# Two PSUM banks for the quantised convolution, and a second issuer for the last image's transfers

## The chip, the cores and the metric

The kernel runs on one core of one Trainium2 chip. The time is device microseconds of one execution of the whole kernel. The core has five engines with instruction streams of their own: TensorE (PE in the profile; its weight loads are the row PEld), VectorE (DVE), ScalarE (ACT), GpSimd (POOL) and SyncE (SP). PE writes its results into PSUM, which here is handled as eight banks of 512 float32 per partition. Transfers between device memory (HBM) and on-chip memory (SBUF) run on 16 DMA engines and are started by an instruction on an engine's queue; in this kernel SP and POOL start them.

## The reference

The input is x, 32 images of 8 channels by 256 by 256 pixels, float32. Four layers follow each other, and each is added to its own input, normalised over groups of two channels:

```python
def _gn(v, G=4, eps=1e-5):
    g = v.reshape(B_, G, C_ // G, H_, W_)
    m = jnp.mean(g, axis=(2, 3, 4), keepdims=True)
    s = jnp.var(g, axis=(2, 3, 4), keepdims=True)
    return ((g - m) / jnp.sqrt(s + eps)).reshape(v.shape)

def _L0_conv_ref(x, K_local, Wp, bp, Wu, bu, Wg1, bg1, Wg2, bg2):
    drive = x[:, :C_OUT]
    grid = drive
    for _ in range(STEPS):                                   # 15
        mapped = R * grid * (1.0 - grid)
        local = _conv(mapped, K_local, groups=C_OUT)         # 3x3, each channel by itself
        physics = (1.0 - EPS) * mapped + EPS * local
        grid = (1.0 - BETA) * physics + BETA * drive
    cml_out = jnp.clip(grid, 0.0001, 1.0 - 0.0001)
    h = jax.nn.relu(_conv(x, Wp, bp))                        # 3x3, 8 -> 128 channels
    nca_out = jax.nn.sigmoid(_conv(h, Wu, bu))               # 1x1, 128 -> 8
    gin = jnp.concatenate([x, cml_out, nca_out], axis=1)     # 24 channels
    g = jax.nn.sigmoid(_conv(jax.nn.relu(_conv(gin, Wg1, bg1)), Wg2, bg2))
    return g * cml_out + (1.0 - g) * nca_out

def _L1_conv_ref(x, weight, bias):
    sx = MAX_Q / jnp.max(jnp.abs(x))                         # over all 32 images
    sw = MAX_Q / jnp.max(jnp.abs(weight))
    qx, qw = _quantize(x, sx), _quantize(weight, sw)         # round, clip to +-127
    return conv3x3(qx, qw) / (sx * sw) + bias[None, :, None, None]

x = x + _L0_conv_ref(_gn(x), ...)
x = x + _L1_conv_ref(_gn(x), ...)
x = x + conv3x3(_gn(x), weight2) + bias2                     # layer 2, 8 -> 8 channels
x = x + box5x5(_gn(x))                                       # layer 3, each channel by itself
```

Layer 1's scale is a maximum over all images after layer 0, so no image can enter layer 1 before the last one has left layer 0.

## The kernel before, in words

**The order is written by a planner.** The kernel builds a list of operations (class `Op`, L61) and gives each an engine, an estimated cost in us, the operations it comes after, a rank, and where needed a `Hold` (a number of PSUM banks that it takes; a later operation frees them) and a transfer size. `Plan.run` (L97) plays these through a small simulation of the five engines: an engine that comes free takes the ready operation of the lowest rank, PE the one of the lowest rank and due time whose banks are free. The order that comes out is the order in which each engine's instructions are written, layer 0 in one plan and layers 1 to 3 of all images in a second. A cost in an `add` call is therefore no instruction: it is an estimate that decides the order. What the chip then does is held in that order by each engine's queue, and between engines by semaphores.

**Layer 0 (to about 9411 us).** An image is worked on as four strips of 64 rows, and strip n = 4 x image + s. For each image 15 steps of the coupled map run on PE (L564), DVE (L587) and ACT (L666), and then:

- the clipped map is written to a buffer `cm_d` in HBM by 76 small stores (L708, through `pool_dma`, L390), 19 rows of tiles by two column sets by two parities, each of 5 to 8 rows of an exchange pattern;
- `hidden` (the 8 to 128 convolution): two loads of `zx` per strip (L770), eight groups of PE matmuls (L810), relu on ACT (L818) and DVE (L824), then the 1x1 convolution (L847, the operation `second`) and its sigmoid (L859) into `nh`, which four stores write to `nn_d` (L864);
- `gate`, one per strip: it reads four loads of `ci` (the map again, L897), `xc` (L908), two loads of `zg` (the input, L920), eight loads of `zc` from `cm_d` and eight of `zn` from `nn_d` (`load_z`, L737). Each load of `load_z` is 16 rows of 8316 bytes, with the source taken as 2 by 8 of them. Its three groups of matmuls (L954) take zg, zc and zn in this order; then relu, a 1x1 matmul, sigmoid, the mixing on DVE, statistics, and two stores to `x1_d`.

zc, zn, zg, ci and xc have one buffer each, so the loads of a gate begin when the gate before has released them. A gate of strip s needs nn of strips s - 1, s and s + 1. All transfers named here are issued by POOL. While the maps of earlier images run, strips of the image before fill the gaps; for the last image, 31, nothing comes after it, and layer 0 ends with its strips 124 to 127.

**Layers 1 to 3 (from about 9411 us).** An image lies in SBUF as 128 partitions of 16 rows. Image after image goes through

- `load1` (L1174): eight loads of x on POOL;
- `layer1`: four `shift` copies on ACT (L1239), rounding on DVE (L1135 and L1136), four `whole` copies on ACT (L1245) that write the rounded image `qh`; two transfers of neighbour rows `qb` on SP (`beside`, L1205); eight convolution groups `conv3` of one bank each (L1190 and L1194), each evicted on ACT into `x2` (L1273) and followed on DVE by the residual and `bn_stats` (L1285, L1294). I call these eight c0 to c7;
- `layer2`: group sums by two small PE operations and DVE work, among them `spread`; four transfers of neighbour rows `xb2` on SP (`beside` again, seen as `xb<-x` at L1205), one buffer of it for all images; four groups of products of two banks (L1367), here P.0 to P.3, evicted on ACT (L1379), statistics (L1391), and copies to a second layout `zz` on POOL (L1406, L1414);
- `layer3`: two groups of products on z and two and a part on zz (L1468, L1474), here Z and ZZ, evicted on ACT (L1493, L1499) into `o`, and 32 stores of `out` per image on SP (L1514).

Layers 1 and 2 take their banks from the first half of PSUM (banks 0 to 3), layer 3 from the second. In layer 1 a convolution group waits for `near` (the rounded image with its neighbour rows) and for the last readers of the `x2` buffer it will be evicted to, that of two images before:

```python
m = add(
    "PE", 0.9, lambda h=hold, i=i: conv3(slot(h), i), near + at_b(x2_used, b - 2),
    takes=hold,
)
```

Its eviction waits for the same readers. So up to four groups may be ahead of the evictions, as many as the half has banks. SP's queue carries in each image, in the order that the plan writes, two qb, the 32 stores of out of the image before, and four xb.

Of the kernel before, what the change touches and what calls it, by code (L numbers as in the profile page):

```python
# [19 lines left out]
C = 8  # L20
# [8 lines left out]
WS = W2 + 2  # L29
SC = WS * WS  # L30
# [175 lines left out]
def window(ap, offset, dims):  # L206
    return bass.AP(ap.tensor, ap.offset + offset, [list(d) for d in dims])
# [3 lines left out]
def kernel(  # L211
# [4 lines left out]
    nc = tc.nc  # L216
# [86 lines left out]
    with ExitStack() as es:  # L303
# [84 lines left out]
        def pool_dma(to, src, after, size, rank=1):  # L388
            return add(
                "POOL", 0.62, lambda: nc.gpsimd.dma_start(to(), src()), after, rank, size=size  # L390
            )

        def sp_dma(to, src, after, rank=0, size=0.2):
            return add(
                "SP", 0.58, lambda: nc.sync.dma_start(to(), src()), after, rank, size=size
            )


        stored_cm, free_a, free_s, set_of = {}, {}, {}, {}
        drive_b, drive_a, begun, tiles = {}, {}, {}, {}  # L400
# [225 lines left out]
        def steps(b):  # L626
# [67 lines left out]
            for q in range(4):  # L694
                cm_at[b][q] = []
                for i in range(5 if q < 3 else 4):
                    ready = [clipped[p, i // 3] for p in range(2)]
                    for e in range(2):
                        for par in range(2):
                            first, count = 2 - par, 7  # L700
                            if not par and q == i == 0:
                                first, count = 0, 8
                            if q and i == 0:
                                first, count = 6 - par, 5
                            if par and q == 3 and i == 3:
                                count = 8
                            at = 33 * q + 7 * i + (first + 1) // 2
                            cm_at[b][q].append(pool_dma(  # L708
                                lambda e=e, par=par, at=at, count=count: window(
                                    cm_d[b % 3], plane(e, par) + at * WS + 1 - e,  # L710
                                    [[WS, count], [SC, C], [1, wide]],
                                ),
                                lambda q=q, i=i, e=e, first=first, count=count: window(
                                    xb, (32 * q + 16 * (1 - e) + first) * row + i * WS,
                                    [[2 * row, count], [5 * WS, C], [1, wide]],
                                ),
                                ready + was, moving(8 * count, 516, 8),
                            ))
                stored_cm[b] += cm_at[b][q]
# [5 lines left out]
        def load_z(name, d, n, after):  # L725

            b, s = divmod(n, 4)
            out = []
            for r in range(2):
                for e in range(2):  # L730
                    for par in range(2):
                        def do(r=r, e=e, par=par):
                            if (r, e, par) == (0, 0, 0):
                                tiles[name, n] = zp.tile([P, 16, WS], F32, name=name, bufs=1)
                            at = 64 * r + 32 * e + 16 * par
                            z = tiles[name, n].rearrange("p s w -> p (s w)")
                            nc.gpsimd.dma_start(  # L737
                                z[at : at + 16, 0 : 16 * WS - 1],
                                window(
                                    d[b % 3], plane(1 - e, par) + (32 * s + 16 * r) * WS + e,  # L740
                                    [[WS, 2], [SC, C], [1, 16 * WS - 1]],
                                ),
                            )

                        out.append(add(
                            "POOL", 0.62, do, after + out[:1], size=moving(16, 8320)
                        ))
            return out

        def at_n(d, n):  # L750
# [10 lines left out]
        def hidden(n):  # L761
# [102 lines left out]
                closed.append(add("ACT", 0.69, close, [w], 0, frees=[hold]))  # L864
            was = [o for m in range(4 * (b - 3), 4 * (b - 2)) for o in at_n(nn_read, m)]
            for q in range(4):
                stored_nn[n].append(pool_dma(
                    lambda q=q: pairs(nn_d[b % 3], s, q), lambda q=q: nhs[n % 3][32 * q : 32 * q + 32],
                    closed + was, moving(256, 520),
                ))  # L870
            if s > 0:
# [16 lines left out]
        def gate(n):  # L888
# [2 lines left out]
            cms = [o for q in range(max(s - 1, 0), s + 1) for o in cm_at[b][q]]  # L891
            ci = []
            for q in range(4):
                def load_ci(q=q):
                    if q == 0:
                        tiles["ci", n] = hp.tile([P, 8, WS], F32, name="ci", bufs=1)
                    nc.gpsimd.dma_start(  # L897
                        tiles["ci", n][32 * q : 32 * q + 32], pairs(cm_d[b % 3], s, q)
                    )

                ci.append(add(
                    "POOL", 0.62, load_ci, cms + at_n(gate_done, n - 1) + ci[:1],
                    size=moving(256, 520),
                ))

            def load_xc():
# [185 lines left out]
    with ExitStack() as es:  # L1092
# [141 lines left out]
        def layer1(b, loaded):  # L1234
            near = []
            for k in range(4):
                def shift(k=k):
                    tiles["tq", b, k] = two.tile([P, 1024], F32, name="tq")
                    nc.scalar.activation(  # L1239
                        tiles["tq", b, k], tiles["x1", b][:, bass.ts(k, 1024)], AF.Identity,  # L1240
                        bias=less1[:, b : b + 1], scale=stat1[:, b, 1:2],
                    )

                def whole(k=k):
                    nc.scalar.activation(  # L1245
                        window(
                            qh, 4 * k * WP + 1, [qh.ap[0], [1, 2], [WP, 4], [2, W2]],
                        ),
                        tiles["tq", b, k].rearrange("p (e i w) -> p e i w", e=2, w=W2),
                        AF.Copy, bias=-ROUND,  # L1250
                    )

                a = add("ACT", 1.1, shift, loaded[k] + at_b(tq_used, 0)[-2:-1] + shifts[-1:])
                shifts.append(a)
                a = add("DVE", 1.55, lambda k=k: round_off(tiles["tq", b, k], sc[:, 0:1]), [a])
                a = add("ACT", 1.1, whole, [a] + at_b(qh_used, b - 1) + at_b(tq_used, 0)[-1:])
                tq_used.setdefault(0, []).append(a)
                near.append(a)
            near += beside(lambda: qb, lambda: qh, ((0, RB - 1, -1), (24, 0, 1)), near, 0.95)
            qh_used[b] = []  # L1260
            ops, last = [], None
            for i in range(NCH):
                hold = Hold(1, 0)
                m = add(
                    "PE", 0.9, lambda h=hold, i=i: conv3(slot(h), i), near + at_b(x2_used, b - 2),
                    takes=hold,
                )
                qh_used[b].append(m)

                def evict(h=hold, i=i):  # L1270
                    if i == 0:
                        tiles["x2", b] = two.tile([P, HB, WP], F32, name="x2")
                    nc.scalar.activation(  # L1273
                        tiles["x2", b][:, 2 * i : 2 * i + 2, 1 : 1 + W],
                        slot(h).rearrange("p (k w) -> p k w", w=W), AF.Identity, bias=b1_sb,
                        scale=sc[:, 3:4],
                    )

                def rest(i=i):
                    if i == 0:  # L1280
                        part_sums[1, b] = few.tile([P, HB, 6], F32, name="bn1")
                    x1, x2 = tiles["x1", b], tiles["x2", b]
                    c = x2[:, 2 * i : 2 * i + 2, 1 : 1 + W]
                    by = window(x2, 2 * i * WP + 1, [x2.ap[0], [1, 2], [WP, 2], [2, W2]])
                    nc.vector.tensor_tensor(  # L1285
                        by, by,
                        window(
                            x1, 1024 * (i // 2) + 2 * W2 * (i % 2),
                            [x1.ap[0], [512, 2], [W2, 2], [1, W2]],
                        ),  # L1290
                        ALU.add,
                    )
                    for n in range(2):
                        nc.vector.bn_stats(part_sums[1, b][:, 2 * i + n, :], c[:, n, :])  # L1294

                last = add("ACT", 0.8, evict, [m, last] + at_b(x2_used, b - 2), 0, frees=[hold])
                ops.append(add("DVE", 1.6, rest, [last] + ops[:1]))
            x1_used[b] = ops
            return sums_of(1, b, ops)
# [120 lines left out]
        def layer3(b, s, a, copies):  # L1420
# [32 lines left out]
            for n in range(2):  # L1453
# [54 lines left out]
                for d in range(4):  # L1508
                    for ro in range(4):
                        u = 1 if n == 1 and d == 0 and ro < 2 else 0  # L1510
                        r = 8 * d + (-2 if n else 2) + ro + 32 * u
                        mine.append(add(
                            "SP", 0.42,
                            lambda n=n, d=d, ro=ro, u=u, r=r: nc.sync.dma_start(  # L1514
                                window(
                                    out, (b * C * H + r) * W, [[H * W, C], [32 * W, 8], [1, W]]
# [252 lines left out]
```

## Time and profile before

| | |
|---|---|
| time, median of 3 runs | 11946.05 us (11938.4 to 11969.75) |
| the profiled execution's own time, and its span | 11955.15 us, 11953.3 us |
| layer 0, layers 1 to 3 | to about 9411 us, 9411 to 11953 us |
| busy share of the span: PE, PEld, DVE, ACT, POOL | 82%, 36%, 57%, 47%, 35% |
| PE in the slices of layer 0, of layers 1 to 3 | eight tenths or nine, five or six tenths |
| granted TensorE clock, mean | 0.921 |
| DMA queues: POOL's (q0), SP's (q1) | 1256.7 MB, 277.6 MB |

The profile is of one execution. Its time is 9.1 us above the median of the three runs, so a sum made from the profile is compared with 11955.15 and then shifted. Times within the profile count from the start of the span. In the lines of a timeline stand the start, the length, the engine (SPq is SP's queue), the source line, the operation, what it writes and reads, the tile's shape and count, and in brackets the idle time of the engine before it with what ended it. In the windows view the columns are the window, its length, then for PE, PEld, DVE, ACT and POOL the busy time with the number of instructions, then the granted clock, the busy share of the DMA engines and their GB/s. In the view of waits stand what is waited for, the sum in us, the number of waits and the longest of them.

### The profile page before, as it was taken

What the parts mean: (1) busy time and instruction counts of PE and PEld (TensorE: products, weight loads), DVE (VectorE), ACT (ScalarE), POOL (GpSimd) and SP (SyncE); (2) the same over time, 40 slices, a digit from 0 to 9 for tenths busy, and PEclk for the clock granted to TensorE, in tenths of its full rate; (3) what the DMA queues carried; (4) which work ended last, traced back from release to release, by engine and by line L of the source; (5) the groups of instructions that cost most, each with busy time, mean ns of one, the idle gap of its engine ahead of it and who ended that gap; (6) DMA issues with size and microseconds to landing.
All of it is one profiled execution on the core that took longest, in us unless ns stands there. A gap on an engine that the chain in (4) does not pass through costs nothing. (4 is left out here: it accounts for less than half of the span.)

```text
span 11953.3 us, 421615 instructions
## 1 busy us (share of the span) xinstructions
PE 9758.7 (82%) x189064; PEld 4300.9 (36%) x189064; DVE 6753.8 (57%) x11601; ACT 5595.9 (47%) x4448; POOL 4136.7 (35%) x7211
## 2 busy tenths in 40 slices
PE   6788989888888888888888888888988556666556
PEld 3334444434444344444444344444444122222122
DVE  5666666666666666666666666666665433333332
ACT  4455555555555555555555555555554333333332
POOL 1334444444444444444444344344444411111110
PEclk9999999999999999999999999999999777877777
DMA  3445555555555555555555555555554555444454
GB/s 116 126 134 138 138 136 144 151 138 137 138 140 140 138 142 138 136 143 144 137 142 140 137 136 142 135 140 139 137 135 112 137 109 109 107 107 105 105 110 83
DMA packets 839913, 1561.23 MB, mean 131 GB/s; under 512 B 425943, under 2 KB 543287, under 8 KB 777687
## 3 DMA queue, kind: packets, MB, share of 16 engines
q0 software_dynamic: 621280, 1256.70, 39.2%
q1 hardware_dynamic: 216831, 277.57, 10.7%
q8 instruction: 1490, 24.41, 0.9%
q14 instruction: 312, 2.56, 0.1%
HBM read 987.19 MB, written 276.55 MB: 106 GB/s over the span
## 5 line engine op out<-in xcount | busy, mean ns | idle before, releaser
L666 ACT ACTIVATE state<-state,edge_sb 128x1556 f32<-128x1556 f32 (+3 forms) x1792 | 2426.8, 1375 | 2545.2 <-DVE state L587 2227.5
L810 PE MATMUL bank<-zx,wpi 32*128 32x512 f32 x24576 | 2916.0, 619 | 400.0 <-DVE state L587 181.5
L564 PE MATMUL bank<-state,wma_sb 32*32 32x387 f32 (+1 forms) x65536 | 1860.7, 456 | 282.3 <-DVE state L587 101.4
L818 ACT ACTIVATE hh<-bank,bi 128x1536 f32<-128x1536 f32 x1024 | 1576.5, 1540 | 1053.4 <-PE bank L810 1053.2
L810 PEld LDWEIGHTS bank<-zx,wpi 32*128 32x128 f32 x24576 | 1283.5, 192 | 1848.1 <-issue 1234.7
L587 DVE SCALAR_TENSOR_TENSOR state<-bank,xa 128x1552 f32<-128x1552 f32 (+1 forms) x896 | 1336.8, 1499 | 970.2 <-PE bank L564 938.9
L564 PE MATMUL bank<-state,wmb_sb 32*32 32x384 f32 x57344 | 1623.5, 449 | 236.9 <-DMA state<-state 94.1
L587 DVE SCALAR_TENSOR_TENSOR state<-bank,xb 128x1556 f32<-128x1556 f32 (+1 forms) x896 | 1328.3, 1503 | 712.0 <-PE bank L564 639.8
L390 POOL DMA_DIRECT2D cm_d<-xb x2432 | 1392.4, 581 | 535.0 <-DVE xb L655 515.1
L564 PEld LDWEIGHTS bank<-state,wma_sb 32*32 32x32 f32 x65536 | 964.8, 104 | 1204.7 <-issue 445.3
L564 PEld LDWEIGHTS bank<-state,wmb_sb 32*32 32x32 f32 x57344 | 884.8, 104 | 982.4 <-issue 397.7
L824 DVE TENSOR_SCALAR hh<-bank,bi 128x512 f32<-128x512 f32 x1024 | 764.5, 747 | 779.1 <-PE bank L810 774.8
L847 PE MATMUL bank<-hh,wu_sb 128*32 128x512 f32 x8192 | 934.8, 596 | 80.5 <-ACT hh L818 64.4
L1367 PE MATMUL bank<-xb,w2i 64*32 64x512 f32 x2048 | 232.9, 699 | 870.6 <-DMA xb<-x 870.6
L737 POOL DMA_DIRECT2D zc<-cm_d x1024 | 569.5, 572 | 512.2 <-DMA zc<-cm_d 182.6
L1406 POOL DMA_DIRECT2D zz<-z x256 | 126.2, 500 | 1791.9 <-ACT z L1379 970.2
L737 POOL DMA_DIRECT2D zn<-nn_d x1024 | 564.9, 561 | 522.4 <-DMA zg<-in_xzg 174.5
L1379 ACT ACTIVATE z<-bank,got 128x1024 f32<-128x1024 f32 x128 | 142.8, 1116 | 1200.4 <-PE bank L1367 1200.4
L390 POOL DMA_DIRECT2D x_d<-xc x256 | 194.4, 801 | 978.9 <-DVE xc L1016 868.9
L390 POOL DMA_DIRECT2D nn_d<-nh x512 | 301.3, 594 | 615.5 <-ACT nh L859 299.2
L847 PEld LDWEIGHTS bank<-hh,wu_sb 128*32 128x32 f32 x8192 | 240.3, 110 | 710.2 <-issue 482.0
L1367 PE MATMUL bank<-x,w2i 64*32 64x512 f32 x6144 | 420.6, 637 | 33.0 <-DVE u L278 24.8
(177 smaller groups left out, 9401.8 us busy)
## 6 DMA issues: line engine op xcount, KB each, us to landing
zx<-in_xzx POOLq DMA_DIRECT2D x256, 520.0 KB
zg<-in_xzg POOLq DMA_DIRECT2D x256, 520.0 KB
zn<-nn_d POOLq DMA_DIRECT2D x1024, 129.9 KB
zc<-cm_d POOLq DMA_DIRECT2D x1024, 129.9 KB
xa<-in_xsa POOLq DMA_DIRECT2D x63, 1300.0 KB
xb<-in_xsb POOLq DMA_DIRECT2D x63, 1300.0 KB
nn_d<-nh POOLq DMA_DIRECT2D x512, 130.0 KB
ci<-cm_d POOLq DMA_DIRECT2D x512, 130.0 KB
```

The lines of the kernel that those rows point to most:

```text
L390: "POOL", 0.62, lambda: nc.gpsimd.dma_start(to(), src()), after, rank, size=size
L564: nc.tensor.matmul(t[32 * q : 32 * q + 32, 512 * g : 512 * g + n * WS].rearrange("p (i w) -> p i w", w=WS)[:, :, 0:wide], w, state[32 * g ...
L587: nc.vector.scalar_tensor_tensor(drive if k == STEPS - 1 else strips(state, p, i, n, k % 2, wide), t.rearrange("p (k w) -> p k w", w=512)[ ...
L666: nc.scalar.activation(t, t, AF.Square, bias=edge_sb[:, 4:5])
L737: nc.gpsimd.dma_start(z[at : at + 16, 0 : 16 * WS - 1], window(d[b % 3], plane(1 - e, par) + (32 * s + 16 * r) * WS + e, [[WS, 2], [SC, C] ...
L810: nc.tensor.matmul(t[:, bass.ts(q, 512)].rearrange("p (k w) -> p k w", w=W2), f["wp"][part, par, dx, :], z[part, of, 4 * v : 4 * v + 4, at ...
L818: nc.scalar.activation(hh[0][:, 0:SHARE], slot(hold)[:, 0:SHARE], AF.Relu, bias=f["bi"][:, 0:1],)
L824: nc.vector.tensor_scalar(hh[0][:, SHARE:], slot(hold)[:, SHARE:], f["bi"][:, 0:1], 0.0, ALU.add, ALU.max,)
L847: nc.tensor.matmul(pn[32 * q : 32 * q + 32, :], wu_sb[:, u, :], hh[:, bass.ts(q, 512)], start=k == 0, stop=k == 3,)
L1367: nc.tensor.matmul(t[32 * d : 32 * d + 32, bass.ts(h, 512)].rearrange("p (k w) -> p k w", w=W), w[part, d % 2, dx, :], z, start=dx == 0, s ...
L1379: nc.scalar.activation(zs[b % 2][:, 4 * j : 4 * j + 4, 2 : 2 + W].rearrange("p (i h) w -> p h i w", h=2), slot(hold).rearrange("p (h i w) ...
L1406: lambda n=n, k=k, to=to, at=at, far=far: nc.gpsimd.dma_start(zz[64 * k + to : 64 * k + to + 32, 8 * n + far : 8 * n + far + 8], zs[b % 2] ...
```

## The change

Three things are changed.

1. In layer 0 a new helper `any_dma` takes the place of `pool_dma` for the stores of cm, the loads of zc and zn, the stores of nn and the loads of ci. For images 0 to 30 it is `pool_dma`. For the last image, b = B - 1, it hands the transfers in turn to `sp_dma` (the first, third, ...) and `pool_dma`. The loads of zx, zg and xc and the stores of x1 stay with POOL.
2. In layer 1 a convolution group no longer waits for the readers of x2 two images before, but for the eviction of the group two before it (`turns[-2:-1]`): while one group is being evicted and another is computed, no third bank is taken. The eviction keeps its wait for x2.
3. Two planner costs: the `whole` copy 1.1 to 1.4, the store of out 0.42 to 0.69.

```diff
+        turn = [0]
+
+        def any_dma(b, to, src, after, size):
+
+            turn[0] += 1
+            return (sp_dma if b == B - 1 and turn[0] % 2 else pool_dma)(
+                to, src, after, size=size, rank=1
             )
...
-                            cm_at[b][q].append(pool_dma(
-                                lambda e=e, par=par, at=at, count=count: window(
+                            cm_at[b][q].append(any_dma(
+                                b, lambda e=e, par=par, at=at, count=count: window(
...
-                        out.append(add(
-                            "POOL", 0.62, do, after + out[:1], size=moving(16, 8320)
-                        ))
+                        out.append(any_dma(b, to, of, after + out[:1], moving(16, 8320)))
...
-                stored_nn[n].append(pool_dma(
-                    lambda q=q: pairs(nn_d[b % 3], s, q), lambda q=q: nhs[n % 3][32 * q : 32 * q + 32],
+                stored_nn[n].append(any_dma(
+                    b, lambda q=q: pairs(nn_d[b % 3], s, q), lambda q=q: nhs[n % 3][32 * q : 32 * q + 32],
                     closed + was, moving(256, 520),
                 ))
...
-                ci.append(add(
-                    "POOL", 0.62, load_ci, cms + at_n(gate_done, n - 1) + ci[:1],
-                    size=moving(256, 520),
+                ci.append(any_dma(
+                    b, to, lambda q=q: pairs(cm_d[b % 3], s, q),
+                    cms + at_n(gate_done, n - 1) + ci[:1], moving(256, 520),
                 ))
...
-                a = add("ACT", 1.1, whole, [a] + at_b(qh_used, b - 1) + at_b(tq_used, 0)[-1:])
+                a = add("ACT", 1.4, whole, [a] + at_b(qh_used, b - 1) + at_b(tq_used, 0)[-1:])
...
-            ops, last = [], None
+            ops, last, turns = [], None, []
...
-                    "PE", 0.9, lambda h=hold, i=i: conv3(slot(h), i), near + at_b(x2_used, b - 2),
+                    "PE", 0.9, lambda h=hold, i=i: conv3(slot(h), i), near + turns[-2:-1],
...
                 last = add("ACT", 0.8, evict, [m, last] + at_b(x2_used, b - 2), 0, frees=[hold])
+                turns.append(last)
...
                         mine.append(add(
-                            "SP", 0.42,
+                            "SP", 0.69,
```

`sp_dma` (L395) is the same call on `nc.sync`, with a planner cost of 0.58 where `pool_dma` has 0.62.

More of the change, by code (lines that the diff above doesn't have):

```diff
@@ L396, in sp_dma @@
             )
+        turn = [0]
[3 more added lines that the diff above has]
+                to, src, after, size=size, rank=1
+            )
         stored_cm, free_a, free_s, set_of = {}, {}, {}, {}
@@ L731, in load_z, with to @@
                     for par in range(2):
-                        def do(r=r, e=e, par=par):
+                        def to(r=r, e=e, par=par):
                             if (r, e, par) == (0, 0, 0):
@@ L736, in do, with of @@
                             z = tiles[name, n].rearrange("p s w -> p (s w)")
[L737 to L742, printed above, removed]
-                            )
-                        out.append(add(
-                            "POOL", 0.62, do, after + out[:1], size=moving(16, 8320)
-                        ))
+                            return z[at : at + 16, 0 : 16 * WS - 1]
+                        def of(r=r, e=e, par=par):
+                            return window(
+                                d[b % 3], plane(1 - e, par) + (32 * s + 16 * r) * WS + e,
+                                [[WS, 2], [SC, C], [1, 16 * WS - 1]],
+                            )
+                        out.append(any_dma(b, to, of, after + out[:1], moving(16, 8320)))
             return out
@@ L893, in gate, with to @@
             for q in range(4):
-                def load_ci(q=q):
+                def to(q=q):
                     if q == 0:
                         tiles["ci", n] = hp.tile([P, 8, WS], F32, name="ci", bufs=1)
-                    nc.gpsimd.dma_start(
-                        tiles["ci", n][32 * q : 32 * q + 32], pairs(cm_d[b % 3], s, q)
-                    )
-                ci.append(add(
-                    "POOL", 0.62, load_ci, cms + at_n(gate_done, n - 1) + ci[:1],
-                    size=moving(256, 520),
+                    return tiles["ci", n][32 * q : 32 * q + 32]
+                ci.append(any_dma(
+                    b, to, lambda q=q: pairs(cm_d[b % 3], s, q),
+                    cms + at_n(gate_done, n - 1) + ci[:1], moving(256, 520),
                 ))
```

## The prediction

> **What bounds the kernel now.** The windows view comes first. Layer 0 (to about 9411 us) keeps TensorE near nine tenths busy until its tail; layers 1 to 3 (9411 to 11953) do not, so I look into one image of them.
>
> ```profile
> 10990.00:11007.00 17.00, 0.00 (x0) 0.00 (x0) 4.44 (x16) 0.19 (x1) 4.73 (x8) 0.52 0.72 125
> 11007.00:11019.00 12.00, 1.88 (x2) 0.18 (x2) 0.00 (x0) 0.00 (x0) 0.00 (x0) 0.50 0.46 115
> 11019.00:11026.00 7.00, 6.69 (x80) 2.11 (x88) 3.40 (x8) 1.12 (x1) 0.00 (x0) 0.58 0.13 46
> ```
>
> For 29 us all five engines stand, with the DMA engines at work. The waits of layers 1 to 3 say for what: layer 2's neighbour rows xb, 846 us in all.
>
> ```profile
> PE bank L1367 <- DMA xb<-x: 845.8, 59, 22.8
> ```
>
> Why xb comes late is read from SP's timeline (start, length, what).
>
> ```profile
> 11033.42 1.39 SPq L1205 DMA_DIRECT2D qb<-qh  x2
> 11036.41 34.67 SPq L1514 DMA_DIRECT2D out<-o  x32
> 11071.19 10.02 SPq L1205 DMA_DIRECT2D xb<-x  x4
> 11111.98 1.39 SPq L1205 DMA_DIRECT2D qb<-qh  x2
> 11118.15 30.98 SPq L1514 DMA_DIRECT2D out<-o  x32
> 11149.25 9.17 SPq L1205 DMA_DIRECT2D xb<-x  x4
> 11188.20 1.39 SPq L1205 DMA_DIRECT2D qb<-qh  x2
> 11191.20 35.88 SPq L1514 DMA_DIRECT2D out<-o  x32
> 11227.19 10.17 SPq L1205 DMA_DIRECT2D xb<-x  x4
> ```
>
> xb is issued within 0.15 us of the end of the 32 stores of out, in every image: SP's own queue is the bound, as a ring. xb lands and TensorE restarts (11019.31, 11098.66, 11177.97, 11254.6); layer 2's first group and layer 3 of the image before run; their evictions free the stores; then xb of the next image goes out, and lands 27 to 29 us later. Over the 27 turns from 9695.1 to 11798.0 a turn takes 77.9 us. Layer 2's last group of an image ends 13 to 17 us before SP reaches xb, so it is not what binds.
>
> The turns are of three kinds, by what stands between layer 2's first group P.0 and layer 3's Z. The PE timeline shows two restarts:
>
> ```profile
> 11098.66 1.96 PE L1367 MATMUL bank<-xb,w2i 64*32 64x512 f32 x14 [8.21 <-DMA xb<-x]
> 11177.97 1.95 PE L1367 MATMUL bank<-xb,w2i 64*32 64x512 f32 x14 [9.63 <-DMA xb<-x]
> ```
>
> After the first, P.1 follows before Z, and the stores begin 19.5 us after the restart; after the second Z follows at once, and they begin at 13.2. Each of the nine turns of this second kind gives 74.9 to 77.2 us, mean 76.3; the other eighteen average (2102.9 - 687)/18 = 78.7. The early start gains less than its 3 to 6 us because SP's second and third store stall until the two qb transfers just ahead are through: the fourth store starts 8.4 us after the first qb (11033.42 to 11041.8; 11188.20 to 11196.65). From the fourth store to the end it takes 29.1 us in all kinds (28.1 to 30.4). So a turn is set by when qb goes, and qb waits for the last rounding copy of L1245 on ScalarE:
>
> ```profile
> 11186.77 1.40 ACT L1245 ACTIVATE qh<-tq 128x1024 bf16<-128x1024 f32 x1
> 11190.06 1.12 ACT L1499 ACTIVATE o<-bank,more 128x1024 f32<-128x1024 f32 x1 [0.61 <-PE bank L1474]
> ```
>
> The tail of layer 0 is read from POOL's timeline: 76 stores of cm stand ahead of the zx loads, TensorE needs zx, and the row of PE shows the wait.
>
> ```profile
> 9228.81 23.61 POOL L390 DMA_DIRECT2D cm_d<-xb  x42 [35.66 <-DVE xb L655]
> 9253.29 18.91 POOL L390 DMA_DIRECT2D cm_d<-xb  x34 [0.87 <-issue]
> 9272.19 0.59 POOL L770 DMA_DIRECT2D zx<-in_xzx  x1
> ...
> 9282.72 0.58 POOL L770 DMA_DIRECT2D zx<-in_xzx  x1
> ```
>
> ```profile
> 9289.75 12.85 PE L810 MATMUL bank<-zx,wpi 32*128 32x512 f32 x96 [16.85 <-DVE zx L779]
> ...
> 9391.12 3.66 PE L954 MATMUL bank<-zn,wg_sb 64*32 64x512 f32 x30 [2.09 <-DMA zn<-nn_d]
> ```
>
> **The change, part by part.** The sum is made against the profiled execution, 11955.15 us (span 11953.3); the median of the three runs is 9.1 us lower.
>
> *cm by turns.* 38 of the 76 stores stay on POOL (38 x 0.57 = 22 us, 9229 to 9251), 38 go on SP, idle there, at about 0.72 each (its stores of out, unhindered: 0.68 and 0.04 between) until 9256. The zx issue comes 21 us earlier, the second zx no longer behind four nn stores; it lands 7 us after issue (9282.72 to 9289.75), well before TensorE is free at 9272.9. The wait of 16.85 us goes.
>
> *The loads and stores of the last four gates.* zc and zn have eight issues each, 4.6 us on POOL; halved they save about 2 us a gate, and nn and the nearer zn loads a little more. Three gates in a row hang on zn: from the buffer's release to the last landing it takes 19.5 us (9309.2 to 9328.7) and 19.2 us (9372.0 to 9391.1). That is what SP's half must beat. What is not shown before is a z load by SP. SP's transfers here post as many completion packets as they have outer rows:
>
> ```profile
> DMA packets 306, 0.34 MB, mean 28 GB/s; under 512 B 80, under 2 KB 192, under 8 KB 304
> q1 hardware_dynamic: 304, 0.31, 10.1%
> ```
>
> Ten exchanges of 8 rows post 80 small packets; ten of 8, 6, 2, 6 and 6 rows, between 9195 and 9209 us, posted 56. A z load has 16 rows against a source whose outer step has 2. If it is spread as POOL's are, the gates give 13 us more, and the tail -30. If two DMA engines carry each, its 130 KB at 62 engine-us per MB (10.1% of 16 engines x 12 us for 0.31 MB) take 4.0 us, one behind the other: seven in a row and 2 us to land make 30 us against 19.5. Those legs lose 10.8 us twice, the middle gate 3.9, one group of L810 moved behind a gate 2.8: +28, which with the first gate held up eats the 16.85 and leaves the tail at +28. Packets alone take 0.31 us (8 x 0.31 = 2.5 us a load), which would leave -11. I take 2.9 us a load, near the low row since little else runs there: -3. The ends -30 and +28 are kept.
>
> *Store cost and rounding cost in the planner (0.42 to 0.69, 1.1 to 1.4).* No instruction is added; they move the order. In the changed build SP's order per image is the same (32 stores, four xb, two qb), but TensorE's order becomes one pattern from image 3 on: P.0, Z and ZZ of the image before, P.1, two conv groups, P.2, the spread, P.3, six conv groups. So all 27 turns become the second kind. On ScalarE both last rounding copies now stand between the evictions of Z's two groups. Z's first group is evicted at about 7.4 to 8.5 us after the restart, two copies of 1.4 us end at 11.35; qb goes then, against 10.9 on average in the nine turns: +0.45 us. A turn costs 76.3 + 0.45 = 76.75, so 27 x (77.9 - 76.75) = 31 us. The x loads of L1174 come some 9 us later than now, beside xb's second half; three turns with no x loads had xb land 26.0 to 26.8 us after issue against 27.6, so this is worth between -1 and +1 us a turn; I take 0 and keep 27 us either way.
>
> *At most two banks, and the wait on x2 dropped.* The first two conv groups may run before the buffer x2 is free; they hold two banks of half 0 until P.3 is through. P.1, P.2 and P.3 then share the other pair. P.2 waits for nothing (two conv groups, 1.75 us, cover P.1's eviction of 1.12). P.3 waits for P.2's eviction, the spread and the copy out of it, behind 1.41 us of bn_stats: about 3.5 us. P.3 ends at 35 + 1.75 + 2.9 = 39.7 us after the restart (now 35). SP reaches xb at 49: nine us of cover, so I cost it at nothing. If the cover goes, each us costs 27. Behind the waiting PE stand P.3 and six conv groups, whose evictions and x loads slip by 5 us; nothing waits for them before the next restart.
>
> *The start.* Image 1 loses Z0 as cover: now Z0 runs during xb(1)'s flight. Now the stores begin at 9551.8; with P1.0, P1.1 first they begin about 6 us later, and image 2 loses 1 more: +7 (0 to +11).
>
> Sum: -31 + 7 - 3 = -27: 11928 for the profiled execution, 11919 as a median. That is 0.23%; about 0.3%, 36 us, is what a measurement can tell from no change.
>
> **Rivals.**
> Halved tail: z loads by SP are no slower than POOL's. For it: POOL's issue time is on the path of each gate. Against: the count of completion packets. -24 - 30 = -54: 11892.
> Two-engine tail: as bounded above, +28 - 24 = +4: 11950. The Trainium skill ("DMA: Bandwidth & Descriptors", section on why a DMA increments its semaphore by 16) states a rule of this kind: the number of engines divides both outer dimensions, and from SP it is always the lowest-numbered ones; by that rule the time would be this rival's, and the counts 80 and 56 agree.
> No gain per turn: qb or xb comes 1.15 us later than I work out, by the later x loads on the same engines. For it: the nine early turns scatter by 2.3 us. +7 - 3: 11950.
> Slower: P.3 becomes the bound. If P.1, P.2 and P.3 each wait 4 us more for a bank, P.3 ends at 39.7 + 12 = 51.7, 2.7 past the stores' end at 49, and xb waits for it: a turn of 76.75 + 2.7 = 79.45, 27 x (79.45 - 77.9) + 7 - 3 = +46: 11992. It decides from 9 us more than I count. For it: two pairs become one; against: the evictions take 1.12 us each.
>
> **How the numbers follow.** Main case 0.37 (11919, own range 11895 to 11943); halved tail 0.22; two-engine tail 0.16; no gain 0.12; slower 0.13. The range reaches from below the halved tail to above the two middle rivals: 11878 to 11966. Faster than 11910: nearly all of the halved tail and two fifths of the main case, with a little of the two-engine one, 0.38. Slower than 11982: 0.10 of the slower case, and 0.01 of the rest. Within: 0.51.
>
> **What would show it.** PE at about 9273 goes on to L810 with no wait for zx, and the time from there to the last stats of layer 0 (9410.3) tells the z loads: a zn wait longer than 19 us on SP is the two-engine tail. In layers 1 to 3 the stores should begin 12.7 to 13.3 us after every restart, the fourth 19.5 to 20, the turn should be 76.5 to 77, and L1367's wait for xb should fall by some 30 us in all. I am wrong if xb no longer follows the last store at once, or if P.3 ends after it.

## The result and the profile after

The changed kernel takes 11898.66 us in the median of 20 runs (11870.34 to 11938.23), the kernel before 11947.9 us (also 20 runs, 11925.94 to 11974.25). The ratio is 0.9958 with a 95% interval of 0.9949 to 0.9967: 50 us faster, with 39 and 61 as the ends. The forecast was 11919 within 11878 to 11966.

The profiled execution of the changed kernel took 11938.23 us, the slowest of its 20; its span is 11936.4. So the two traces lie only 17 us apart, and they are best compared stage by stage. I cut them at two points that TensorE's timeline gives in every kernel: the end of the third-last `second` (9272.9 before, 9294.2 after), and the last small statistics matmul of layer 0 (9410.6 before, 9449.1 after). All times of the table are us from the traces; a turn is the mean over the 27 restarts from image 3 to image 30. The experiments of the next section stand in it too.

| kernel | up to the tail | tail of layer 0 | layers 1 to 3 | one turn |
|---|---|---|---|---|
| before | 9272.9 | 137.7 | 2542.8 | 77.9 |
| after | 9294.2 | 154.8 | 2487.4 | 76.2 |
| transfers of image 31 alone | 9287.8 | 160.0 | 2545.3 | 78.0 |
| layers 1 to 3 alone | 9247.0 | 138.2 | 2496.0 | 76.6 |
| changed, only cm by turns | 9269.2 | 125.8 | 2488.0 | 76.1 |
| changed, SP's z loads in halves | 9276.2 | 133.2 | 2476.0 | 75.9 |
| before, xb by POOL | 9274.0 | 135.4 | 1879.2 | 56.0 |
| layers alone, xb by POOL | 9259.5 | 140.4 | 1936.8 | 58.0 |

The first column differs by up to 27 us between the four kernels with an identical layer 0 (9247.0 in "layers alone", 9274.0 in "before, xb by POOL"). That is the scatter of a single execution. The 21 us by which the changed kernel is late there are no effect of the change: at the first transfer that the change moves, a store of nn that starts at 9192.0 before and at 9211.9 after, it is 20 us late already. The other two columns scatter too, but less: the tail takes 135.4 to 140.4 us in those four kernels, and the four kernels with the changed layers 1 to 3 take 2476.0 to 2496.0 us for them. Both effects are clear of that: the tail became 17 us longer, layers 1 to 3 became 55 us shorter.

**Layers 1 to 3.** SP's timeline of the changed kernel, the same stretch as shown of before (start, length, what):

```profile
10967.60 1.41 SPq L1210 DMA_DIRECT2D qb<-qh  x2
10969.37 35.06 SPq L1520 DMA_DIRECT2D out<-o  x32
11004.55 11.63 SPq L1210 DMA_DIRECT2D xb<-x  x4
11042.27 1.41 SPq L1210 DMA_DIRECT2D qb<-qh  x2
11044.04 33.07 SPq L1520 DMA_DIRECT2D out<-o  x32
11077.22 12.82 SPq L1210 DMA_DIRECT2D xb<-x  x4
```

xb is still issued within 0.15 us of the last store. What moved is when the chain begins. Averaged over the 27 turns, in us after the restart: the second qb goes at 11.7 (before 13.3), the first store behind it at 13.0 (16.3), the fourth at 19.6 (21.0), xb at 47.6 (50.3); layer 2's last group ends at 40.2 (35.4). From the fourth store to xb it takes 28.0 us, where it took 29.2. xb then lands 28.7 us after its issue (27.6). ScalarE's timeline shows the order that the prediction names: both rounding copies between the evictions of Z's two groups.

```profile
11038.61 1.11 ACT L1505 ACTIVATE o<-bank,more 128x1024 f32<-128x1024 f32 x1 [4.56 <-PE bank L1480]
11039.62 2.62 ACT L1250 ACTIVATE qh<-tq 128x1024 bf16<-128x1024 f32 x2
11042.90 1.11 ACT L1505 ACTIVATE o<-bank,more 128x1024 f32<-128x1024 f32 x1 [0.66 <-PE bank L1480]
```

In the page of the profile, the group of layer 2's products that reads xb waits for it 683.6 us in all, 187 less than before (870.6). That is far more than the turns gained: 27 times the 4.8 us by which P.3 now ends later is 130, and 44 is the gain of the turns. Most of this fall is TensorE's waiting moved to an earlier place in the same turn.

```profile
L1367 PE MATMUL bank<-xb,w2i 64*32 64x512 f32 x2048 | 232.9, 699 | 870.6 <-DMA xb<-x 870.6
```

```profile
L1373 PE MATMUL bank<-xb,w2i 64*32 64x512 f32 x2048 | 227.1, 701 | 683.6 <-DMA xb<-x 683.6
```

The first line is of the kernel before, the second of the changed one.

**The tail of layer 0.** TensorE's timeline, from the group that waited 16.85 us for zx before:

```profile
9295.07 10.58 PE L817 MATMUL bank<-zx,wpi 32*128 32x512 f32 x96 [0.84 <-ACT nh L866]
...
9320.47 3.66 PE L959 MATMUL bank<-zc,wg_sb 64*32 64x512 f32 x30 [5.34 <-DMA zc<-cm_d]
...
9328.30 3.66 PE L959 MATMUL bank<-zn,wg_sb 64*32 64x512 f32 x30 [1.84 <-DMA zn<-nn_d]
...
9359.30 3.66 PE L959 MATMUL bank<-zn,wg_sb 64*32 64x512 f32 x30 [6.02 <-DMA zn<-nn_d]
...
9429.82 3.66 PE L959 MATMUL bank<-zn,wg_sb 64*32 64x512 f32 x30 [2.22 <-DMA zn<-nn_d]
```

The wait for zx is gone, and waits for zc and zn stand in its place. The waits of TensorE in the tail, summed, of the kernel before and then of the changed kernel (us, times, longest):

```profile
PE bank L954 <- DVE zg L757: 21.9, 2, 16.2
PE bank L810 <- DVE zx L779: 16.8, 1, 16.8
PE bank L954 <- DMA zn<-nn_d: 6.2, 5, 2.3
```

```profile
PE bank L959 <- DMA zc<-cm_d: 25.3, 6, 5.7
PE bank L959 <- DVE zg L764: 14.5, 1, 14.5
PE bank L959 <- DMA zn<-nn_d: 10.1, 3, 6.0
```

Before, there was no wait for zc at all, and zn was waited for 6.2 us in all. Why the loads are late is seen in a stretch in which SP's z loads have the DMA engines nearly to themselves, 9320 to 9324 us, in the view of the DMA queues:

```profile
DMA packets 52, 0.20 MB, mean 50 GB/s; under 512 B 28, under 2 KB 28, under 8 KB 28
q1 hardware_dynamic: 26, 0.20, 11.9%
```

24 of the 26 packets on SP's queue are rows of 8316 bytes (52 less the 28 small ones). They keep 11.9% of 16 engines busy, 1.9 engines, and a load of 16 rows takes 16/24 x 4 = 2.7 us. Over the whole tail the packets tell the same: of the 512 such rows on SP's queue at most two are under way at once (three for 0.3 us in all), while of the 512 rows of the same loads on POOL's queue up to 13 are.

### The profile page after: what moved, and what is told of

Same layout as the page of the kernel before. It is cut to its first block, busy times and chain, and to the rows that moved or that the text cites. A ratio compares the mean times of both kernels' runs of the same rounds, so it can differ in the third digit from the quotient of the medians.

```text
span 11936.4 us, 421674 instructions
## 1 busy us (share of the span) xinstructions
PE 9834.0 (82%) x189064; PEld 4325.1 (36%) x189064; DVE 6751.1 (57%) x11601; ACT 5586.8 (47%) x4448; POOL 4083.5 (34%) x7125
## 5 line engine op out<-in xcount | busy, mean ns | idle before, releaser
L1373 PE MATMUL bank<-xb,w2i 64*32 64x512 f32 x2048 | 227.1, 701 | 683.6 <-DMA xb<-x 683.6
L1397 DVE BATCH_NORM_STATS2 bn<-z 128x6 f32<-128x256 f32 x512 | 179.8, 414 | 792.8 <-ACT z L1385 792.8
```

Of the source, the lines that this page charges most:

```text
L1373: nc.tensor.matmul(t[32 * d : 32 * d + 32, bass.ts(h, 512)].rearrange("p (k w) -> p k w", w=W), w[part, d % 2, dx, :], z, start=dx == 0, s ...
```

## Experiments

Where times of the kernel before are given, they are of the same job on the same chip: 11959.91 us for the first four experiments, 11956.61 for the last two. Gains in us are worked out from the ratio in the first four, and are differences of the medians in the last two; the two ways differ by up to 8 us.

**The transfers of image 31 alone.** Is the tail a loss or a gain?

```diff
-                a = add("ACT", 1.4, whole, [a] + at_b(qh_used, b - 1) + at_b(tq_used, 0)[-1:])
+                a = add("ACT", 1.1, whole, [a] + at_b(qh_used, b - 1) + at_b(tq_used, 0)[-1:])
...
-                    "PE", 0.9, lambda h=hold, i=i: conv3(slot(h), i), near + turns[-2:-1],
+                    "PE", 0.9, lambda h=hold, i=i: conv3(slot(h), i), near + at_b(x2_used, b - 2),
...
-                            "SP", 0.69,
+                            "SP", 0.42,
```

> The kernel before with only the transfers of image 31 by turns; layer 1 and the planner's costs as before. Two-engine theory (a z load by SP runs on two DMA engines: in the changed kernel's trace 24 rows of 8316 bytes in 4 us, 11.9% of 16 engines): the wait for zx at the tail is gone, but the gates wait for zc and zn, the tail is 17 us longer and the whole 15 to 20 us slower, ratio 1.0014. Rival (the tail is a gain and the profiled execution's layer 0 was long for another reason): 15 to 30 us faster, ratio 0.998. In layers 1 to 3 both expect the turns of before, 77.9 us.

Measured: 11991.14 us, ratio 1.0020 (1.0012 to 1.0029), 24 us slower, with 14 and 35 as the ends. The tail is 160.0 us long against 137.7, the turn 78.0 us. The waits of TensorE in this kernel's tail are much like those of the changed kernel:

```profile
PE bank L959 <- DMA zc<-cm_d: 23.6, 6, 6.2
PE bank L959 <- DVE zg L764: 21.8, 2, 19.1
PE bank L959 <- DMA zn<-nn_d: 11.9, 3, 6.4
```

So the first part of the change, alone, makes the kernel slower.

**Layers 1 to 3 alone.** The two-bank rule and both costs, with the tail of before.

```diff
-                a = add("ACT", 1.1, whole, [a] + at_b(qh_used, b - 1) + at_b(tq_used, 0)[-1:])
+                a = add("ACT", 1.4, whole, [a] + at_b(qh_used, b - 1) + at_b(tq_used, 0)[-1:])
...
-                    "PE", 0.9, lambda h=hold, i=i: conv3(slot(h), i), near + at_b(x2_used, b - 2),
+                    "PE", 0.9, lambda h=hold, i=i: conv3(slot(h), i), near + turns[-2:-1],
...
-                            "SP", 0.42,
+                            "SP", 0.69,
```

> The kernel before with only the two-bank rule of layer 1 and the two planner costs; the tail of layer 0 as before. Two-engine theory: all of the gain and more, 50 to 60 us faster, ratio 0.9953, thus faster than the changed kernel by some 15 us; turns of 76.3 us. Rival (the tail is a gain): 25 to 35 us faster, ratio 0.9975, slower than the changed kernel.

Measured: 11892.14 us, ratio 0.9950 (0.9936 to 0.9964), 60 us faster. Turns of 76.6 us, layers 1 to 3 in 2496.0 us, tail 138.2. The sum of the two halves, 24 - 60 = -36, agrees with the -50 of the whole within their intervals. That this kernel is faster than the changed one is not told by the two ratios, whose intervals overlap. It is likely from the tail, which is 16.6 us shorter, more than the scatter of some 5 us; layers 1 to 3 are the same in both.

**Only cm by turns.** The changed kernel, in which the loads of zc, zn and ci and the stores of nn stay on POOL.

```diff
-            turn[0] += 1
-            return (sp_dma if b == B - 1 and turn[0] % 2 else pool_dma)(
+            turn[0] += cm
+            return (sp_dma if cm and b == B - 1 and turn[0] % 2 else pool_dma)(
...
-                                ready + was, moving(8 * count, 516, 8),
+                                ready + was, moving(8 * count, 516, 8), True,
```

> The changed kernel, but only the 76 stores of cm go by turns; the loads of zc, zn and ci and the stores of nn of image 31 stay with POOL. Two-engine theory: no wait for zx, no z load on SP, so the tail is some 10 to 17 us shorter than before instead of 17 longer, and the whole 65 to 75 us faster than before, ratio 0.994. Rival (SP's late start on cm, 34 us for 38 stores, is what delays the gates): the first zc still comes late, the tail is no shorter than before, ratio 0.9955.

Measured: 11884.86 us, ratio 0.9938 (0.9927 to 0.9950), 74 us faster. The tail takes 125.8 us, 12 less than before and 29 less than in the changed kernel. In its timeline of TensorE the zx group starts at once, and the second gate's last zn load lands 19.5 us after zn's buffer is free (9295.9 to 9315.47), as before:

```profile
9270.06 10.58 PE L817 MATMUL bank<-zx,wpi 32*128 32x512 f32 x96 [0.83 <-ACT nh L866]
...
9293.95 1.95 PE L959 MATMUL bank<-zn,wg_sb 64*32 64x512 f32 x30 [2.07 <-DMA zn<-nn_d]
...
9315.47 3.31 PE L959 MATMUL bank<-zn,wg_sb 64*32 64x512 f32 x30 [3.12 <-DMA zn<-nn_d]
```

SP's late end with cm (34 us for 38 stores in the changed kernel) is in this kernel too, with 36 us, and so is not what lengthens the tail.

**SP's z loads in halves.** The changed kernel; each z load that SP issues is cut in two of 8 rows, so its source has one outer step of 8 instead of two steps of 2 and 8. The rows and bytes are the same.

```diff
-                                d[b % 3], plane(1 - e, par) + (32 * s + 16 * r) * WS + e,
-                                [[WS, 2], [SC, C], [1, 16 * WS - 1]],
+                                first = plane(1 - e, par) + (32 * s + 16 * r + (h or 0)) * WS + e
+                                rows = [[WS, 2]] if h is None else []
+                                d[b % 3], first, rows + [[SC, C], [1, 16 * WS - 1]],
```

> The changed kernel, but each load of zc and zn that SP issues is cut into two of 8 rows, whose source has one outer step of 8 instead of two steps of 2 and 8. Two-engine theory (the shape of a load by SP decides how many engines carry it): 8316-byte packets on SP's queue now keep about 8 engines busy instead of 1.9, the gates no longer wait 20 us for zc and zn, and the tail is 15 to 30 us shorter than in the changed kernel, ratio to before 0.9935. Rival (the load is slow because of SP's queue, whatever its shape): no better than the changed kernel, 0.9958, or a little worse for twice as many issues.

Measured: 11884.85 us, ratio 0.9940 (0.9926 to 0.9953), 72 us faster. The tail takes 133.2 us, 22 less than in the changed kernel, with twice as many z loads on SP. The DMA queues in the second gate's loads, 9311 to 9315 us:

```profile
DMA packets 297, 0.83 MB, mean 208 GB/s; under 512 B 197, under 2 KB 197, under 8 KB 197
q0 software_dynamic: 215, 0.47, 52.2%
q1 hardware_dynamic: 81, 0.36, 41.2%
```

SP's queue now keeps 41.2% of 16, 6.6 engines, busy, and up to eight of its rows of 8316 bytes are under way at once. With the same queue, rows and bytes, the shape of the load made the difference. It does so on SP's queue: POOL's loads have the first shape, and up to 13 of their rows are under way at once in the changed kernel. The rule that the prediction named, of the Trainium skill ("DMA: Bandwidth & Descriptors", section on why a DMA increments its semaphore by 16), gives two engines for the first shape and eight for the second; 1.9 and 6.6 busy engines, and two and eight rows at once, agree with it. Which engines they are no run here shows. Even so the halves are no better than leaving these loads with POOL: with cm alone by turns the tail takes 125.8 us, 7 less than here, and the whole takes the same time.

**xb by POOL.** Is the ring through SP's queue really what sets the turn? The kernel before, with the four transfers of xb per image issued by POOL. Nothing else is changed by hand, but the planner orders around it.

```diff
-        def beside(t, src, rows, after, size):
+        def beside(t, src, rows, after, size, engine="SP"):
...
-                    "SP", 0.7,
-                    lambda to=to, r=r, k=k: nc.sync.dma_start(
+                    engine, 0.7,
+                    lambda to=to, r=r, k=k: (nc.sync if engine == "SP" else nc.gpsimd).dma_start(
...
-                ((0, RB - 1, -1), (32, 8, 0), (64, 7, 0), (96, 0, 1)), [a] + at_b(near_used, b - 1), 1.95,
+                ((0, RB - 1, -1), (32, 8, 0), (64, 7, 0), (96, 0, 1)), [a] + at_b(near_used, b - 1), 1.95, "POOL",
```

> The kernel before, but the four transfers of xb in each image are issued by POOL instead of SP; nothing else is changed by hand, the planner reorders around it. Ring theory (xb only waits for its turn in SP's queue, behind the last store): xb is issued right after layer 2's last group, some 35 to 42 us after the restart instead of 50.3, and a turn falls from 77.9 to about 66 to 72 us, so the whole is 150 to 300 us faster, ratio 0.975 to 0.987. Rival (the DMA engines are the bound, and xb issued earlier only lands later, beside the stores): the turn stays at 76 us or more, ratio 0.995 to 1.0.

Measured: 11292.05 us (11276.91 to 11294.37), ratio 0.9438 (0.9425 to 0.9450): 665 us faster, more than twice what the theory gave at most. All of it is in layers 1 to 3 (1879.2 us instead of 2542.8); a turn takes 56.0 us. Two lines of POOL's timeline, and three of SP's:

```profile
10526.68 2.26 POOL L1205 DMA_DIRECT2D xb<-x  x4 [7.55 <-PE bank L1367]
...
10583.06 2.26 POOL L1205 DMA_DIRECT2D xb<-x  x4 [7.27 <-PE bank L1318]
```

```profile
10507.00 1.43 SPq L1205 DMA_DIRECT2D qb<-qh  x2
10509.23 51.06 SPq L1514 DMA_DIRECT2D out<-o  x32
10562.92 1.43 SPq L1205 DMA_DIRECT2D qb<-qh  x2
```

xb now leaves 0.4 us after layer 2's last group of the image before, at 10526.3 and 10582.7, while the stores of out go on until 10560. A turn gains 21.9 us. Some 6 to 7 of it are a quicker landing: 19.4 to 22.4 us from issue to restart wherever TensorE goes straight into the wait, against 27.6. SP needed 9 to 10 us to issue the four transfers behind its stores, POOL 2.3. Most of the rest is the earlier issue, 33 to 39 us after the restart in these turns, against 50.3. The rival, which put a turn at 76 us or more, is refuted by the 56.0; the windows over these layers show the room that the DMA engines had, in the kernel before and then in this one (after the window and its length: PE, PEld, DVE, ACT and POOL busy, granted clock, DMA share, GB/s):

```profile
9434.00:11930.00 2496.00, 1516.37 (x20078) 534.06 (x20085) 929.16 (x2687) 810.23 (x860) 294.22 (x533) 0.78 0.50 106
```

```profile
9434.00:11270.00 1836.00, 1472.54 (x20157) 551.15 (x20157) 930.24 (x2686) 809.58 (x862) 365.28 (x660) 0.89 0.75 144
```

The DMA engines were half idle; they are now busy for 0.75 of the time. TensorE is granted a clock of 0.89 instead of 0.78 in these layers, and its busy time falls by 44 us. The wait for xb falls to 205.8 us from 846:

```profile
PE bank L1367 <- DMA xb<-x: 205.8, 39, 10.0
```

**The two-bank rule and the costs, with xb by POOL.**

The edit is the diff of "layers 1 to 3 alone" and that of "xb by POOL" together, shown here in part:

```diff
-                    "PE", 0.9, lambda h=hold, i=i: conv3(slot(h), i), near + at_b(x2_used, b - 2),
+                    "PE", 0.9, lambda h=hold, i=i: conv3(slot(h), i), near + turns[-2:-1],
...
-                ((0, RB - 1, -1), (32, 8, 0), (64, 7, 0), (96, 0, 1)), [a] + at_b(near_used, b - 1), 1.95,
+                ((0, RB - 1, -1), (32, 8, 0), (64, 7, 0), (96, 0, 1)), [a] + at_b(near_used, b - 1), 1.95, "POOL",
```

> The two-bank rule and the two costs (tail of layer 0 as before), and xb issued by POOL. Ring theory: as with the kernel before, 150 to 300 us faster than before; but since layer 2's last group now sets when xb goes, the 4.8 us by which the two-bank rule delays that group (40.2 against 35.4 us after the restart) counts, and this kernel is no better than the one with xb by POOL alone, or up to 130 us slower than it. Rival (DMA engines are the bound): 0.995, as without POOL.

Measured: 11356.61 us (11338.44 to 11368.13), ratio 0.9493 (0.9480 to 0.9505): 600 us faster than before, but 64.6 us slower than the same with the layers of before. A turn takes 58.0 us. With the ring gone from SP's queue, the edits that gained 60 us cost 65. The theory had said so, but its reason, P.3's later end, is not what the traces show: P.3 ends 33 to 36 us after the restart in the ordinary turns here, and 33 to 37 with the layers of before. The ordinary turns are as long, too, 56.2 us on average against 56.6. What differs are pairs of a long turn, at whose end xb has landed before TensorE comes to it (32 to 38 us from issue to restart), and a short one: here seven pairs of 119.3 us on average, there five of 109.6. Why this order makes more of them, and longer ones, stays open.

**Left open.** The two-bank rule alone and the two planner costs alone gave no measured time, so which of them brings the gain of layers 1 to 3 is not settled. In the orders that the planner writes, the two-bank rule alone already gives the one pattern with the early Z on TensorE, and keeps xb behind all 32 stores; the costs alone leave TensorE's patterns mixed, but put xb ahead of the last one, three or six stores. Either could be part of it. xb by POOL together with cm by turns, which should be faster still by the 12 us of the tail, was not tried.

## Why the prediction was right, and where it was not

The time lies in the range, and in the main case's own range of 11895 to 11943, but that is in part luck, for it owes this to two errors of opposite sign: the tail was put at -3 and is +17, layers 1 to 3 at -24 and are -55. The direction, faster by more than 0.3%, had a chance of 0.38 and "within" 0.51.

*What bounds the kernel.* Right, and shown: taking xb off SP's queue gave 665 us. The bound was described too narrowly, though. The landing of 27 to 29 us was taken as given, and it fell to 19.4 to 22.4 us with POOL, which issues the four transfers in 2.3 us where SP took 9 to 10.

*The turn.* All 27 turns became the second kind, as worked out, at 76.2 us instead of 76.75: 44 us instead of 31. The chain up to the fourth store came as forecast: the stores begin at 13.0 (I had 12.7 to 13.3), the fourth goes at 19.6 (19.5 to 20). Mis-sized were the two terms behind it, which nearly cancel. From the fourth store to xb it takes 28.0 us instead of the 29.1 that I had taken from before, for a reason that no run shows, so xb goes 1.4 us earlier than my 49; and it lands 1.1 us later than my 27.6. This last is the upper bound that I had kept for the later x loads (-1 to +1), and the mechanism of the rival "no gain per turn"; the x loads do begin later, at 57.4 us after the restart instead of 50.5. That they cause the later landing is not shown by a run of its own, but the turns without them fit: xb landed 25.2, 25.3 and 24.6 us after issue in the three last turns. TensorE's wait for xb, which I had falling by some 30 us, fell by 187: I had left out there that P.3's later end shortens this wait by as much as it lengthens the work before it.

*The start.* I counted +7; from the end of layer 0 to image 3's restart it took 277.9 us against 284.5, so -6.6. The failed step is "SP's order per image is the same". The counts are, but not the places: the new cost of a store puts the third xb ahead of six stores and the fourth ahead of twelve. SP's timeline of the changed kernel:

```profile
9593.86 31.33 SPq L1520 DMA_DIRECT2D out<-o  x26
9625.30 11.35 SPq L1210 DMA_DIRECT2D xb<-x  x4
9636.70 16.75 SPq L1520 DMA_DIRECT2D out<-o  x6
...
9676.68 23.53 SPq L1520 DMA_DIRECT2D out<-o  x20
9700.33 11.14 SPq L1210 DMA_DIRECT2D xb<-x  x4
9711.52 21.42 SPq L1520 DMA_DIRECT2D out<-o  x12
```

The turn from image 2 to 3 then took 72.0 us instead of 79.9. The end of the kernel, from image 30's restart, gave another 4.5 us (150.8 against 155.3), which I had not counted.

*The two-bank wait.* Right: P.3 ends 40.2 us after the restart (39.7 forecast) and nothing waits for it, since SP reaches xb at 47.6. The rival "P.3 becomes the bound" had 7 us left on average, and 0.9 in the closest turn.

*The tail.* The wait for zx went, as said, and the first gate then took it back: from the cut at 9272.9 and 9294.2 its zn ends 36.3 us later before, 37.7 after. The failed term is the 2.9 us a load. Alone, a load takes 2.7; but with POOL's half running beside it, the last zn load landed 27.3 us after the release in the second gate (9332.0 to 9359.3) and 28.4 in the last (9401.5 to 9429.8). Seven loads and 2 us to land make that 3.6 to 3.8 us a load. I had chosen the low row "since little else runs there", and POOL's half of the same loads runs there: in the last gate SP's queue starts 26 rows in the 10 us from 9402 while POOL's loads run, and some six a us after 9413, when they are through. Against the 19.5 and 19.2 us of before, the two gates lose 7.8 and 9.2, together the 17 us that the tail lost. So the rival "two-engine tail" had the mechanism, and at 28 was too high by 11. SP's stores of cm took 0.90 us each, not 0.72, which cost nothing visible.

## What to carry to other kernels

When every stall ends in the same transfer, look at which queue issues it and what stands ahead of it there, before shaving what starts that queue: here the edits of the order were worth 60 us, and giving the transfer to POOL's queue, whose engine was busy for 294 us of the 2496 us of that window, 665. Splitting transfers over two queues is no even split: a load's shape decided whether SP's queue carried it on two DMA engines or on up to eight, and the slower half sets the end. And a planner's cost moves more than the place that it was meant for, so count the places in the written order, not only the number of instructions.

## What was not expected

- Moving xb to POOL shortened not only its wait in the queue: from issue to restart 19.4 to 22.4 us instead of 27.6, and four issues in 2.3 us instead of 9 to 10.
- With less waiting, TensorE's granted clock in layers 1 to 3 rose from 0.78 to 0.89; what that adds to the gain was not separated.
- The same edits of layer 1 and of the costs gained 60 us with xb on SP and lost 65 us with xb on POOL.
